# Holding 36 parts of the table in groups, storing 24 KB rows, and splitting the last step by blocks of the batch

## The chip, the cores and the metric

The kernel runs on one core of a Trainium2 chip. The metric is the device time of one execution in microseconds, the median of several runs. "Profile" means the record of one execution; its times count from the span's start. Engines: PE multiplies, ACT and DVE work on elements, POOL (GpSimd) issues the gathers, SP issues the stores; PSUM is the memory into which PE writes. A "packet" is one entry in the record of the 16 DMA engines; a store has one for each row of a partition, beside entries of 4 bytes that are left out here. The "seam" is the passage from the first stage to the second.

## The reference, cut to what matters

```python
emb = emb_table.at[0].set(0.0)              # 100001 x 128
e = emb[seq]                                # seq: 1024 x 50
prefix = jnp.cumsum(e, axis=1)
uF = prefix / denom[:, :, None]             # min(t, length)
mean, var = uF.mean(axis=0), uF.var(axis=0) # over the batch, for each step
y = (uF - mean) * lax.rsqrt(var + 1e-5) * gamma + beta
def step(v, x):
    v = v + (x - v) / 2.0
    spike = atan_spike(v - 1.0)             # 1 where v >= 1
    return v - spike, spike
_, spikes = lax.scan(step, v0, x_seq)       # 50 steps, in order
scores = spikes.mean(axis=0) @ emb.T        # 1024 x 100001, 410 MB
```

The first stage is the 50 steps: each gathers 1024 rows and ends in a count of spikes. The second multiplies the counts (1024 x 128) by the whole table and writes 410 MB. Almost nothing of it can start before the last step is done.

## The kernel before: the parts that the change touches

The table is cut into 98 "parts" of 1024 rows. A part is loaded (512 KB, 4 KB a partition), transposed by PE, split into a high and a low half (`hi`, `lo`; the result is the sum of two products), multiplied with eight blocks of 128 users, scaled out of PSUM by DVE and ACT in turn, and stored.

```python
CH = 4096            # a chunk: four parts, so a 16 KB row in each store
AHEAD = 8            # chunks loaded during the first stage: 32 parts
...
for c, (c0, w) in enumerate(chunks):
    ...
    for n in range(NB):                        # 8 blocks of 128 users
        o = op.tile([P, CH], F32, tag="o")     # three of these
        for q in range(parts[c]):
            ...product..., scale by 1/T into o[:, h0:h0+hw]
            if n == NB - 1: free.append(split.pop((c, q))[2]); ready()
        store(n, c0, o[:, :w])                 # on SP's queue
        if n in (2, 5): ready()                # transpose and split a part of the next chunk
    ...
    fetch(ahead.pop(0), rowp)                  # a later chunk, on ACT's queue
```

The last step works in two halves of 512 users, and block A (users 0 to 127) is multiplied first:

```python
x(halves[0]); x(halves[1])          # ACT: scale and shift
upper(0, 3, pt)                     # ACT: high half of part 3
step(halves[0])                     # DVE: 512 columns
spiked(countA, slice(0, P), vt)     # DVE: the counts of block A
for h, po in enumerate(pre):
    product(po, 0, 0, 0, h * BANK, BANK)
step(halves[1]) ...
```

## Time and profile before

| | before |
|---|---|
| time, median of 3 | 1660.91 us |
| span of the profile | 1587.5 us |
| second stage, first store to end | 513.5 to 1587.5 us |
| stored / fetched in the second stage | 409.6 / 34.4 MB |
| stores | 16 KB rows, 2 MB each, 12.8 us from issue to landing |

These are the queues of the page of the kernel before (packets, MB, share of the time of 16 DMA engines); q1 carries the stores and the first loads, q0 the gathers, q10 the fetches of the second stage:

```profile
q1 hardware_dynamic: 36256, 426.67, 63.9%
q0 software_dynamic: 12800, 26.24, 6.1%
q10 hardware_dynamic: 9292, 34.42, 6.1%
```

The prediction shows the rest: POOL paces the first stage, the bytes on the DMA engines the second. PE, at 78 to 85% in the second stage, is not far behind.

The profiled run was 71 us shorter than the timed ones.

### The profile page before, as it was taken

The page shows a single profiled execution, that of the slowest core. Times are in us where ns is not written, and L with a number is a line of the kernel's source. Part 1 is how long each engine was busy: PE and PEld are TensorE (multiplying, and loading weights), DVE is VectorE, ACT ScalarE, POOL GpSimd, SP SyncE. Part 2 cuts the span into 40 slices and gives each one's busy share as a digit, 9 for nine tenths or more (in the row PEclk, how much of TensorE's full clock was granted, in tenths as well). Part 3 has the DMA queues.
Part 4 walks back from the last instruction along what each step waited for, and adds up shares of the span by engine and source line. Part 5 has one row for each costly group of instructions (what it writes and reads, how often), then busy time and mean ns, then how long its engine had stood idle before and what let it go on. Part 6 is the DMA issues. An engine that isn't in the chain of part 4 may idle for free.

```text
span 1587.5 us, 12689 instructions
## 1 busy us (share of the span) xinstructions
PE 1137.8 (72%) x4532; PEld 804.7 (51%) x4532; DVE 939.4 (59%) x1162; ACT 631.6 (40%) x699; POOL 378.4 (24%) x406
## 2 busy tenths in 40 slices
PE   4555555555555977788888878788888788888884
PEld 2222222222233765566666666666666666666663
DVE  4777777777778654555555554555555545555553
ACT  2322222222233544444444444444444444444442
POOL 6777777777775000000000000000000000000000
PEclk9999999999965999999999999999999999999998
DMA  9522122221221999999999999999999999999998
GB/s 341 187 53 53 52 53 53 53 53 52 53 53 51 380 429 426 424 422 415 418 426 407 418 426 422 417 414 415 416 416 419 422 420 411 427 411 412 416 417 345
DMA packets 58410, 488.13 MB, mean 307 GB/s; under 512 B 12491, under 2 KB 13292, under 8 KB 33772
## 3 DMA queue, kind: packets, MB, share of 16 engines
q1 hardware_dynamic: 36256, 426.67, 63.9%
q0 software_dynamic: 12800, 26.24, 6.1%
q10 hardware_dynamic: 9292, 34.42, 6.1%
q8 instruction: 35, 0.57, 0.1%
q14 instruction: 27, 0.22, 0.0%
HBM read 77.69 MB, written 409.60 MB: 307 GB/s over the span
## 4 chain that ended last, share of the span: by engine, by line
DMA 52%; POOL 18%; issue 10%; PE 9%; DVE 7%; ACT 3%; DVEq 0%; SPq 0%; ACTq 0%; POOLq 0%
DMA scores<-o 48%; POOL e L191 18%; PE po L152 8%; DVE o L434 5%; DMA e<-in_L_rec_emb_table,idx 3%; ACT o L436 3%; PE pt L104 1%; PE pre L300 0%; ACT hi L136 0%; DVE s L330 0%; DVE bs L310 0%; DVE uF L309 0%; DMA idx<-in_r_seq 0%; ACT v L345 0%; DVE negv L353 0%
## 5 line engine op out<-in xcount | busy, mean ns | idle before, releaser
L434 DVE TENSOR_SCALAR o<-po 128x1024 f32<-128x1024 f32 x390 | 462.6, 1220 | 442.0 <-DMA scores<-o 338.5
L436 ACT ACTIVATE o<-po 128x1024 f32<-128x1024 f32 (+1 forms) x390 | 385.4, 1018 | 528.2 <-DMA scores<-o 347.4
L191 POOL DMA_INDIRECT e<-in_L_rec_emb_table,idx x400 | 377.7, 944 | 124.6 <-issue 116.4
L152 PE MATMUL po<-hi,countC 128*128 128x512 f32 x624 | 261.0, 418 | 81.7 <-ACT o L436 81.5
L300 PE MATMUL pre<-ident,e 128*128 128x128 f32 x400 | 155.9, 451 | 146.9 <-DMA e<-in_L_rec_emb_table,idx 145.0
L152 PE MATMUL po<-lo,countC 128*128 128x512 f32 x624 | 248.9, 399 | 0.0
L152 PE MATMUL po<-hi,countB 128*128 128x512 f32 x468 | 192.2, 411 | 14.4 <-ACT o L436 13.9
L300 PEld LDWEIGHTS pre<-ident,e 128*128 128x128 f32 x400 | 79.2, 200 | 241.7 <-DMA e<-in_L_rec_emb_table,idx 219.9
L152 PEld LDWEIGHTS po<-hi,countC 128*128 128x128 f32 x624 | 120.2, 193 | 133.5 <-ACT o L436 110.7
L152 PE MATMUL po<-lo,countB 128*128 128x512 f32 x468 | 186.9, 399 | 0.0
L104 PE MATMUL pt<-ident,rows 128*128 128x128 f32 x782 | 113.2, 292 | 70.5 <-ACT o L436 65.4
L104 PEld LDWEIGHTS pt<-ident,rows 128*128 128x128 f32 x782 | 96.4, 150 | 96.3 <-ACT o L436 79.8
L324 ACT ACTIVATE r<-mv,eps 128x1 f32<-128x1 f32 x50 | 14.8, 295 | 302.8 <-DVE mv L320 302.8
L152 PEld LDWEIGHTS po<-lo,countC 128*128 128x128 f32 x624 | 120.5, 193 | 22.1
L309 DVE SCALAR_TENSOR_TENSOR uF<-rlen,pre 128x512 f32<-128x512 f32 x100 | 68.3, 683 | 105.5 <-PE pre L300 105.5
L140 DVE TENSOR_TENSOR lo<-pt,hi 128x1024 fp32r<-128x1024 f32 x78 | 93.7, 1218 | 40.9 <-ACT hi L136 40.9
L152 PEld LDWEIGHTS po<-hi,countB 128*128 128x128 f32 x468 | 91.6, 196 | 41.7 <-ACT o L436 19.8
L152 PEld LDWEIGHTS po<-lo,countB 128*128 128x128 f32 x468 | 91.1, 195 | 18.2
L152 PE MATMUL po<-more,countC 128*128 128x512 f32 (+1 forms) x320 | 87.7, 413 | 16.1 <-ACT o L436 16.1
L136 ACT CAST hi<-pt 128x1024 fp32r<-128x1024 f32 x78 | 79.0, 1013 | 48.7 <-PE pt L104 48.7
L268 PE MATMUL sums<-s,ident_h 128*128 128x512 bf16 x98 | 49.6, 608 | 61.1 <-DVE s L330 61.1
L257 PE MATMUL pre<-zT,l 128*128 128x512 f32 x100 | 76.9, 771 | 19.7 <-DVE uF L309 19.5
(77 smaller groups left out, 942.7 us busy)
## 6 DMA issues: line engine op xcount, KB each, us to landing
scores<-o SPq DMA_DIRECT2D x190, 2048.0 KB, 12.8
rows<-in_L_rec_emb_table ACTq DMA_DIRECT2D x16, 2048.0 KB, 27.0
rows<-in_L_rec_emb_table SPq DMA_DIRECT2D x8, 2048.0 KB, 26.0
scores<-o SPq DMA_DIRECT2D x8, 848.5 KB, 14.6
e<-in_L_rec_emb_table,idx POOLq DMA_INDIRECT x400, 2.5
scores<-o SPq DMA_DIRECT2D x2, 1024.0 KB, 3.9
scores<-o SPq DMA_DIRECT2D x3, 512.0 KB, 2.7
scores<-o SPq DMA_DIRECT2D x2, 256.0 KB, 2.1
```

The source lines that it names most:

```text
L104: nc.tensor.transpose(pt[:, k0 : k0 + kw], rows[c][:kw, q * KQ + k0 // P, :], ident[:kw, :kw])
L136: nc.scalar.copy(vh, vp)
L140: nc.vector.tensor_tensor(vl, vp, vh.bitcast(F32), ALU.subtract)
L152: nc.tensor.matmul(po[:, :kw], lhsT=counts[n], rhs=part[:, k0 : k0 + kw], start=j == 0, stop=j == 1,)
L191: nc.gpsimd.indirect_dma_start(out=es[t][:, n * P : (n + 1) * P], out_offset=None, in_=table, in_offset=bass.IndirectOffsetOnAxis(ap=idx[: ...
L257: nc.tensor.matmul(pre[h], lhsT=l, rhs=zT[:, h * BANK : (h + 1) * BANK], start=t == 0, stop=False, skip_group_check=True,)
L268: nc.tensor.matmul(sums[h], lhsT=ident_h, rhs=s[:, h * BANK : (h + 1) * BANK], start=t == 0, stop=t == T - 2, skip_group_check=True,)
L300: nc.tensor.matmul(pre[h][:, k : k + P], lhsT=e[:, h * BANK + k : h * BANK + k + P], rhs=ident, start=False, stop=last, is_transpose=True, ...
L309: nc.vector.scalar_tensor_tensor(uF[:, cs], rlen[:, cs], 1.0 / (t + 1), pre[h], ALU.max, ALU.mult)
L324: nc.scalar.activation(r, mv[:, 1:2], AF.Sqrt, bias=eps)
L434: nc.vector.tensor_scalar_mul(o[:, h0 : h0 + hw], po[:, :hw], 1.0 / T)
L436: nc.scalar.mul(o[:, h0 : h0 + hw], po[:, :hw], 1.0 / T)
```

## The change

Its intent is to move fewer bytes in the second stage (36 parts held in place of 32), to move them in longer rows (24 KB), and to get the first store out sooner. To make room, the buffers are laid out as six groups of six parts, which are reused one by one: as pairs for the split halves, as output buffers, as places for later fetches. Chunks start narrow, since at first little room is free.

```diff
-CH = 4096
-AHEAD = 8
+GROUP = 6
+AHEAD = 6
+WIDTHS = [2, 2, 2, 3, 3, 3, 3] + 12 * [6] + [4, 4]
 ...
-                if T - 8 <= t < T - 2 and t % 2 == 0:
+                if t in (T - 8, T - 6):           # two parts prepared early, not three
 ...
-        pt = vp.tile([P, HALF], F32, tag="v0", name="pt_3")
-        turned(0, 3, pt)
-        x(halves[0])
-        x(halves[1])
-        upper(0, 3, pt)
-        step(halves[0])
-        spiked(countA, slice(0, P), vt)
+        warm = vp.tile([P, HALF], F32, tag="v0", name="warm")
+        for k in range(2 * KQ):
+            nc.tensor.transpose(warm[...], ident, ident)
+        vC = vp.tile([P, B - BANK - P], F32, tag="v1", name="vC")
+        groups = [
+            (slice(0, P), pre[0][:, :P], countA),
+            (slice(P, P + BANK), pre[1], countB),
+            (slice(P + BANK, B), vC, countC),
+        ]
+        for cs, vt, _ in groups: x(vt, cs)
+        cs, vt, first = groups[0]
+        step(vt, cs); spiked(first, cs, vt)
+        for cs, vt, _ in groups[1:]: step(vt, cs)
+        for cs, vt, c in groups[1:]: spiked(c, cs, vt)
 ...
-            if n in (2, 5):
+            if 2 <= n < NB - 1:
                 ready()
+            if n in (1, 4) and c >= MIDDLE and to_fetch < parts:
+                ...fetch(r, to_fetch, GROUP // 2)     # 1.5 MB, twice a wide chunk
```

## The prediction

> **What bounds the kernel now.** I read the page first: the 40 slices, the chain that ended last, and the DMA issues.
>
> ```profile
> DMA  9522122221221999999999999999999999999998
> GB/s 341 187 53 53 52 53 53 53 53 52 53 53 51 380 429 426 424 422 415 418 426 407 418 426 422 417 414 415 416 416 419 422 420 411 427 411 412 416 417 345
> ...
> DMA 52%; POOL 18%; issue 10%; PE 9%; DVE 7%; ACT 3%; DVEq 0%; SPq 0%; ACTq 0%; POOLq 0%
> ...
> scores<-o SPq DMA_DIRECT2D x190, 2048.0 KB, 12.8
> rows<-in_L_rec_emb_table ACTq DMA_DIRECT2D x16, 2048.0 KB, 27.0
> rows<-in_L_rec_emb_table SPq DMA_DIRECT2D x8, 2048.0 KB, 26.0
> ```
>
> There are two stages. For the first 13 slices (to about 510 us) the DMA engines are nearly idle after the first 55 us, in which eight chunks of the table are loaded. From slice 14 on they are full, at 407 to 429 GB/s, until the end. A 2 MB store lands 12.8 us after its issue although 2 MB at 420 GB/s take 5 us, so a backlog stands before the DMA engines.
>
> The first stage is paced by GpSimd's gathers. The timeline of that engine is the same at the beginning, under the load, as at its end:
>
> ```profile
> 30.73 0.94 POOL L191 DMA_INDIRECT e<-in_L_rec_emb_table,idx  x1 [0.30 <-issue]
> 31.97 0.94 POOL L191 DMA_INDIRECT e<-in_L_rec_emb_table,idx  x1 [0.30 <-issue]
> ...
> 502.63 0.94 POOL L191 DMA_INDIRECT e<-in_L_rec_emb_table,idx  x1 [0.30 <-issue]
> ```
>
> One gather every 1.25 us, 400 of them, 500 us; "issue" means that it waits for nothing shown. The loaded DMA engines at 30 us don't slow it.
>
> The busy time by stretches of the second stage shows the seam and the rest:
>
> ```profile
> 510.00:520.00 10.00, 7.26 (x24) 5.31 (x25) 7.45 (x11) 3.81 (x6) 0.00 (x0) 0.78 0.38 147
> 520.00:530.00 10.00, 10.00 (x50) 8.32 (x49) 6.09 (x6) 6.04 (x6) 0.00 (x0) 1.00 0.92 376
> ...
> 560.00:800.00 240.00, 187.96 (x841) 146.36 (x840) 123.45 (x106) 103.97 (x106) 0.00 (x0) 0.96 1.01 422
> 800.00:1300.00 500.00, 407.35 (x1776) 316.61 (x1777) 262.50 (x224) 220.84 (x223) 0.00 (x0) 0.95 1.01 418
> 1350.00:1560.00 210.00, 178.75 (x822) 138.94 (x821) 122.34 (x107) 101.13 (x104) 0.00 (x0) 1.00 0.99 417
> ```
>
> The columns are PE, its weight loads, DVE, ACT and POOL busy, then the granted clock, the DMA share and GB/s. DMA is at 0.99 to 1.01 throughout, PE at 78 to 85%, DVE at 51 to 58%. So the second stage lasts as long as its bytes take, and what can shorten it is fewer bytes, cheaper packets, or an earlier start.
>
> The seam itself, in the timeline, where "a" (the scale of the last step) is done at 508.79:
>
> ```profile
> 508.88 1.59 ACT L345 ACTIVATE v<-uF,hgb,a 128x512 f32<-128x512 f32 x2
> 510.42 1.00 ACT L136 CAST hi<-pt 128x1024 fp32r<-128x1024 f32 x1
> 510.51 0.70 DVE L348 SCALAR_TENSOR_TENSOR v<-negv,v 128x512 f32<-128x512 f32 x1 [1.72 <-ACT v L345]
> 511.24 0.29 DVE L279 SCALAR_TENSOR_TENSOR countA<-v,count 128x128 fp32r<-128x128 f32 x1
> ...
> 511.59 0.79 PE L152 MATMUL pre<-hi,countA 128*128 128x512 f32 x1 [3.40 <-DVE countA L279]
> ...
> 513.47 44.45 SPq L161 DMA_DIRECT2D scores<-o  x15
> ```
>
> The first product waits for countA, countA for a step over 512 columns, and that for both activations, although countA needs only 128 columns. The first store is issued at 513.47.
>
> One thing I can't explain: the timed runs take 1660.91 us, the profiled one 1589.44. I take the 71 us as the same for both kernels, so a saving in the profile is a saving in the time.
>
> **What the Trainium skill says.** "DMA: Bandwidth & Descriptors", section "Where 436 GB/s comes from", puts the ceiling of the 16 engines at 435 GB/s; the trace's 417 to 422 are 96% of it. Its section "Why small descriptors are slow (HBM only)" names a fixed cost for each packet. The packet records of this trace agree: medians of 159 ns for 4096 bytes, 311 for 8192 and 611 for 16384, a line of about 9 ns plus 0.0367 ns a byte. "HBM Reference", section "Specifications (TRN2)", gives about 358 GB/s for a core of a busy pair and says that a core alone exceeds it; 420 here is the core alone. "TensorE: Matmul & The Clock Gate", Part 1, says that the clock is halved after an idle window of about 3.4 us and full after a busy one. The clock records agree: half from 487 until 514.5 us, with PE continuously busy only from 511.59, and the products of 128x512 take 0.63 us before and 0.39 after.
>
> **The change, part by part.**
>
> 1. Fewer bytes in the second stage. Before, 8 chunks of 4 parts are loaded in stage one, 66 of 98 parts later. After, 36 parts are held and 62 come later. Four parts of 512 KB are 2.1 MB, at 420 GB/s 5.0 us. The extra bytes move to stage one, where DMA is idle and POOL wasn't delayed by the load: no cost. Gain 5.0 us.
>
> 2. Packets. In the stretch without fetches, 1350 to 1560, 5334 packets of 16384 bytes took 210 us on 16 engines: 630 ns each with the gap, against 602 for the bytes alone at 27.2 GB/s an engine (435/16), so 28 ns fixed. Beside fetches the gaps are filled by the other queue and only some 10 ns of it remain. The widths of the chunks are now 3x2, 4x3, 12x6 and 2x4 parts, with 8, 12, 24 and 16 KB packets. For 24 KB, 12288 packets save half a fixed cost each: 5 ns x 12288 / 16 = 3.8 us beside fetches, 14 ns and 10.8 us without. Eleven of the twelve wide chunks have fetches beside them, so I take 4.5 us. Against it the first seven chunks, none with fetches: 3072 packets of 8 KB cost half a fixed cost more than half a 16 KB packet does, 14 x 3072 / 16 = 2.7 us; 4096 packets of 12 KB a quarter, 7 x 4096 / 16 = 1.8 us. The sum is about nothing: between 3 us gained and 2 us lost. I enter 0.5 us gained.
>
> 3. The last step in three pieces. The activation for A covers 128 columns, about 0.39 us (the 128x128 activation of "l" took that) in place of 1.59 for two halves; the step over 128 columns about 0.29 in place of 0.70. So countA is ready at about 508.88 + 0.39 + 0.2 + 0.3 + 0.1 + 0.29 = 510.1, against 511.53. The order of PE's instructions shows sixteen transposes without use behind the counting matmuls, which end at 506.5: 16 x 0.24 = 3.8 us (eight took 1.91), up to 510.3, just before the first product. The busy window begins earlier, and the full clock should come at 511.1, one 3.4 us window before 514.5. The first store should leave near 511.6 in place of 513.47. After it, n = 0 has two parts in place of four, and PE makes a part in 0.93 us at full clock, faster than the 1.25 us that the DMA engines take to store it. The two stretches 510 to 530 moved 147 x 10 + 376 x 10 = 5.2 MB where 420 GB/s would move 8.4: 7.6 us lost. After, I expect 2 us before the first store and some 1.5 us of ramp. Gain 4 us.
>
> 4. New waits. The first chunks have two parts, and with three pairs of split buffers the second part of the next chunk is only transposed behind the first product of the last block. It needs the transposes (1.9), the cast (1.0) and the subtraction (1.2); PE has two products of 0.93 to cover the last two. That is a stall of about 1 to 2 us at the first two boundaries, at a time when little backlog stands. PE needs 2 x (7.4 + 1.9) = 18.6 us for such a chunk plus the stall, DMA 20: nearly even. Cost 1.5 us. From the third chunk on, five and then ten pairs are free, and the order of instructions shows the splits spread over blocks 2 to 6.
>
> Sum: 5.0 + 0.5 + 4.0 - 1.5 = 8 us in the middle; if gaps between stores beside fetches shrink too, some 4 us more. I take 10, so 1651 us.
>
> **Rivals.** First, PE becomes the bound in chunks 0 to 7, which now have no fetches: 24 parts at 10 us each for DMA, against 9.3 for PE at full clock. The stretch 1350 to 1560 speaks against it: no fetches there, DMA still 0.99, PE 85% busy. If the clock fell to 0.9 as in some stretches of 560 to 1300, PE would need 10.3 and the loss would be 24 x 0.3 = 7 us, leaving the time near 1658. Second, the long packets bring the whole 14 ns (10.8 us), because the queue is deeper with 3 MB stores and never empties: then about 1643. Third, the gain from the fetches is hidden because the held rows take the room of the output buffers, and the early stores of 1 MB don't keep DMA busy: a DMA share of 0.95 over chunks 0 to 6 (180 us) would cost 9 us, and the time would be as before. Fourth, the extra load delays the gathers: against it stands the 1.25 us pace at 30 us.
>
> **Range and chances.** Every term is under 1% of the time and the terms of loss are as large as those of gain, so over 2% (33 us) either way needs something that I don't see, most likely in the unexplained 71 us. Predicted 1651 us, range 1638 to 1662; faster by over 2%: 0.03, within 2%: 0.95, slower by over 2%: 0.02.
>
> **What would show it.** The bytes of the second hardware queue should fall from 34.42 to about 32.3 MB. The first store should leave at 511 to 512, and the clock in 510 to 520 should be above 0.78, with the DMA share of that stretch near 0.7. The DMA share from 520 to 700 should stay at 0.98 or more; if it is 0.95, the third rival is right, and with PE over 92% busy there, the first. The median packet of 24 KB should take about 911 ns. POOL should end at 503.6 as before. I would be wrong altogether if the time moved by more than the profile's span did.

## The result

| | before | after | ratio |
|---|---|---|---|
| | 1660.81 (4 runs) | 1649.11 (4 runs) | 0.9930 (0.9912 to 0.9947) |
| chip 9, run again | 1588.53 (9) | 1576.12 (5) | 0.9919 |
| chip 12, run again | 1589.05 (9) | 1576.17 (5) | 0.9918 |

Ratios are the mean time of one kernel's fast runs over that of the other's of the same rounds, so not quite the ratio of the medians.

The change saves 12 us, under 1%, wherever it is run. The level differs by 72 us between runs on different chips, for both kernels alike: on chips 3, 9 and 12 before takes 1588.5 to 1589.3 us, on chip 8 it takes 1661.1. Each chip was used in one session only, so chip and session can't be told apart; "kind of chip" below means which level was seen. By level, the profile of before came from the first kind, its timed runs and the profile of after from the second. So **the two pages must not be subtracted**: they would say that after is 59 us slower. The waits of POOL show what differs. In the profile of after (waiter, what it waited for, total us, times, longest):

```profile
POOL e L187 <- issue: 109.8, 360, 0.3
POOL e L187 <- remote: 64.2, 16, 4.4
```

On chip 9 the same kernel has the first of these two lines only, 114.0 us in 374 waits. So the gathers stop 16 times for about 4 us, 64 us in all; "remote" means that the profile has no record of what ended the wait. With one more stop of 5.5 us this is nearly the whole 71 us by which the scale of the last step comes later (579.15 against 508.29). The gathers are not where it begins: beside the stop at 79.1 us DVE had waited from 70.4 to 79.72, also for "remote", while POOL went on issuing and PE's eight transposes of that step stand in the record as ended at 71.1. The gathered data was on time (packets from 1.7 to 2.1 us after the issue, beside a stop as elsewhere). What DVE waited for, the record doesn't show. The comparisons below that rest on traces use chip 9, 3 or 12.

The page of after on chip 9, the DMA engines in 40 slices, the queues, and the issues (KB each, us from issue to landing):

```profile
DMA  9612121222121999999999999999999999999998
GB/s 337 249 52 54 52 54 52 54 52 54 52 54 44 391 411 419 420 399 424 424 428 430 430 426 421 422 422 415 425 429 417 416 423 416 430 425 421 384 423 353
...
q1 hardware_dynamic: 31984, 428.77, 64.8%
...
q10 hardware_dynamic: 8844, 32.33, 5.2%
...
scores<-o SPq DMA_DIRECT2D x96, 3072.0 KB, 20.0
...
rows<-in_L_rec_emb_table ACTq DMA_DIRECT2D x20, 1536.0 KB, 29.7
```

The fetches of the second stage fell by 2.1 MB. The second stage is full as before, with two slices that sag: 399 (the 18th, around 690 us) and 384 (the 38th, around 1470). A store now lands 20 us after its issue; three of 3 MB can stand in line.

The stretches of the same profile (PE, weight loads, DVE, ACT, POOL busy, granted clock, DMA share, GB/s):

```profile
510.00:520.00 10.00, 9.51 (x45) 7.57 (x46) 6.64 (x9) 5.82 (x8) 0.00 (x0) 1.00 0.71 279
520.00:530.00 10.00, 9.46 (x45) 7.38 (x44) 7.36 (x7) 5.34 (x6) 0.00 (x0) 1.00 0.93 382
560.00:690.00 130.00, 115.83 (x536) 89.41 (x535) 78.23 (x67) 65.33 (x67) 0.00 (x0) 0.99 1.00 416
690.00:700.00 10.00, 9.35 (x41) 7.43 (x40) 7.98 (x7) 5.57 (x7) 0.00 (x0) 1.00 0.77 322
800.00:1300.00 500.00, 407.96 (x1773) 321.00 (x1772) 261.78 (x222) 218.94 (x222) 0.00 (x0) 0.94 1.00 423
1465.00:1480.00 15.00, 12.05 (x45) 9.15 (x44) 7.09 (x6) 5.93 (x6) 0.00 (x0) 0.89 0.71 304
```

From 510 to 520 the clock is full and the DMA share 0.71, where before had 0.38. In the long stretch of the middle the rate is 423 in place of 418 GB/s. The two dips are in the fourth and the last line.

The seam of after on chip 9, in the timeline:

```profile
508.29 0.27 DVE L335 TENSOR_SCALAR a<-q,r,hgb 128x1 f32<-128x1 f32 x1
508.66 1.17 ACT L339 ACTIVATE pre<-uF,hgb,a 128x128 f32<-128x128 f32 x2
509.15 0.30 DVE L342 SCALAR_TENSOR_TENSOR pre<-negv,pre 128x128 f32<-128x128 f32 x1 [0.59 <-ACT pre L339]
509.49 0.29 DVE L275 SCALAR_TENSOR_TENSOR countA<-pre,count 128x128 fp32r<-128x128 f32 x1
...
509.92 0.47 PE L149 MATMUL sums<-hi,countA 128*128 128x512 f32 x1 [0.44 <-ACT pre L339]
...
510.23 0.40 PE L149 MATMUL sums<-lo,countA 128*128 128x512 f32 x1
...
511.29 0.84 SPq L158 DMA_DIRECT2D scores<-o  x2
```

The same steps of before, on the same chip:

```profile
508.45 0.27 DVE L339 TENSOR_SCALAR a<-q,r,hgb 128x1 f32<-128x1 f32 x1
...
511.52 0.79 PE L152 MATMUL pre<-hi,countA 128*128 128x512 f32 x1 [3.43 <-DVE countA L279]
...
513.41 1.31 SPq L161 DMA_DIRECT2D scores<-o  x2
```

From the start of the scale "a" to the first store it is now 3.0 us; before took 5.0 (508.45 to 513.41). Three quarters of that lie ahead of the first product, which starts 1.6 us after "a" in place of 3.1.

**A balance of the second stage.** I summed the packet records of chip 9's traces from the first store packet to the last one, each divided by 16 engines. Idle is the time in which fewer than 16 packets were in flight, overlap that in which more were; busy plus idle less overlap is the length.

| us | before | after | difference |
|---|---|---|---|
| store packets | 965.5 | 967.1 | +1.6 |
| fetch packets | 95.0 | 80.9 | -14.1 |
| instructions' own loads | 2.2 | 2.2 | 0 |
| idle, first 20 us | 3.2 | 1.8 | -1.4 |
| idle, last 10 us | 4.8 | 4.5 | -0.3 |
| idle, between | 7.2 | 10.2 | +3.0 |
| overlap | -6.9 | -6.0 | +0.9 |
| length | 1071.0 | 1060.8 | -10.2 |

With the first packet 2.1 us earlier (512.14 against 514.27) this is the whole 12.4 us. A second trace of the changed kernel, a1, has 965.9 for the store packets and 10.9 for the idle between, so both of these lines are good to about 1.3 us only; its fetch packets agree to 0.1. The packet means (ns):

| packet | before | after |
|---|---|---|
| store, 8 KB | 318 | 317 |
| store, 12 KB | | 469 |
| store, 16 KB | 617 | 619 |
| store, 24 KB | | 924 |
| fetch, 4 KB | 180.5 | 163.4 |

The long stores are hardly cheaper a byte than those of 16 KB (924 against one and a half times 617, 926). It is the fetch packets beside them that got shorter: 3.1% of their packets took over 400 ns before, 0.6% after.

### The profile page after: what moved, and what is told of

Its sections match the earlier page's. It is cut to its first block, busy times and chain, and to the rows that moved or that the text cites. A ratio compares the mean times of both kernels' runs of the same rounds, so it can differ in the third digit from the quotient of the medians.

```text
span 1646.4 us, 12555 instructions
## 1 busy us (share of the span) xinstructions
PE 1115.2 (68%) x4538; PEld 829.4 (50%) x4548; DVE 940.4 (57%) x1161; ACT 630.6 (38%) x700; POOL 379.3 (23%) x406
## 4 chain that ended last, share of the span: by engine, by line
DMA 48%; DVE 22%; another core or an unknown queue 10%; PE 9%; ACT 5%; issue 4%; POOL 1%; DVEq 0%; ACTq 0%; SPq 0%
DMA scores<-o 48%; PE po L149 8%; ACT o L456 4%; DVE bs L306 4%; DVE uF L305 4%; DVE v L342 3%; DVE s L326 3%; DVE negv L348 3%; DVE o L454 2%; POOL e L187 1%; DVE a L335 1%; DVE mv L316 1%; DVE q L332 0%; PE pt L119 0%
## 5 line engine op out<-in xcount | busy, mean ns | idle before, releaser
L149 PE MATMUL po<-pairs,countB 128*128 128x512 f32 x1168 | 313.9, 415 | 66.8 <-ACT o L456 49.6
L149 PEld LDWEIGHTS po<-pairs,countB 128*128 128x128 f32 x1168 | 225.4, 198 | 131.3 <-ACT o L456 64.4
L149 PE MATMUL po<-pairs,countC 128*128 128x512 f32 x876 | 238.2, 417 | 43.2 <-ACT o L456 43.0
L149 PEld LDWEIGHTS po<-pairs,countC 128*128 128x128 f32 x876 | 168.8, 199 | 89.3 <-ACT o L456 54.8
L305 DVE SCALAR_TENSOR_TENSOR uF<-rlen,pre 128x512 f32<-128x512 f32 x100 | 68.0, 680 | 180.5 <-remote 145.0
L142 DVE TENSOR_TENSOR pairs<-pt,pairs 128x1024 fp32r<-128x1024 f32 (+1 forms) x73 | 88.4, 1217 | 94.7 <-ACT pairs L141 94.7
L149 PE MATMUL po<-hi,countB 128*128 128x512 f32 x200 | 82.9, 414 | 19.2 <-ACT o L456 14.9
L149 PE MATMUL po<-lo,countB 128*128 128x512 f32 x200 | 80.4, 402 | 0.0
L149 PE MATMUL po<-pairs,countA 128*128 128x512 f32 (+1 forms) x292 | 73.5, 393 | 9.1 <-ACT o L456 9.1
L141 ACT CAST pairs<-pt 128x1024 fp32r<-128x1024 f32 (+1 forms) x73 | 73.6, 1008 | 15.0 <-PE pt L119 14.9
L149 PE MATMUL po<-hi,countC 128*128 128x512 f32 x150 | 63.2, 421 | 17.7 <-ACT o L456 17.7
```

Of the source, the lines that this page charges most:

```text
L141: nc.scalar.copy(vh, vp)
L142: nc.vector.tensor_tensor(vl, vp, vh.bitcast(F32), ALU.subtract)
L149: nc.tensor.matmul(po[:, :kw], lhsT=counts[n], rhs=part[:, k0 : k0 + kw], start=j == 0, stop=j == 1,)
L305: nc.vector.scalar_tensor_tensor(uF[:, cs], rlen[:, cs], 1.0 / (t + 1), pre[h], ALU.max, ALU.mult)
```

## The experiments

Each is a run of 5 rounds (before run again: 3) beside the kernel before on the same chip. The changed kernel took 1576.12 us on chip 9 and 1576.17 on chip 12; the differences below are to the first of these, for seam0 to the second. Nowarm, hold30, w4 and tailsp ran on chip 3, where the changed kernel was not run and before took 1589.25, 0.7 us more than on chip 9. Reckoned from before on their own chip, their differences would be 0.7 us smaller: 1.5, 6.0, 4.4 and -0.4 us. So these four are good to about 0.7 us.

### The kernel before, again (b0)

No edit.

> The kernel before, unchanged, to see its trace in the state of the timed runs. The changed kernel's profile has its first store at 582.1 us, with sixteen holes of 2 to 5 us in the gathers of GpSimd; the profile of before (1587.5 us) has no such hole and its first store at 513.5. Theory: in the timed runs (1660.8) the kernel before has the same holes, so a new profile spans about 1659 with the first store near 585 and the stage after it at 1074 us as before. Rival: its first stage is as in the old profile (513 us) and the stores take 1145 us instead, in which case the change would have traded one for the other. Ratio to before 1.000.

Measured: 1588.58 us, ratio 0.9999; its first store at 513.41 us, no hole. Here the state that the question was about was absent, so neither theory was tested. Only chip 8, in use later, brought 1661 us and the holes back; before was not profiled there.

### The changed kernel, again (a0, a1)

No edit; a0 on chip 9, a1 on chip 12.

> The changed kernel, unchanged, as the base for the edits in this call. Theory and rival alike: 1649 us within 2, ratio to before 0.993; first store near 582, 1064 us from there to the end.

> The changed kernel, unchanged, beside the next run, as its base and to see its ratio to before once more: 0.992 to 0.993 in either kind of session (1576 of 1588.5, or 1649 of 1660.8).

Measured: 1576.12 and 1576.17 us, ratios 0.9919 and 0.9918. The level of 1649 and the first store near 582 that were expected of a0 belong to the other kind of chip; the ratio holds on both.

### The last step in halves again (halves)

```diff
-        for cs, vt, _ in groups: x(vt, cs)
-        ...
+        vl = vp.tile([P, B], F32, tag="v1", name="vl")
+        for cs in halves: x(vl[:, cs], cs)
+        step(vl[:, halves[0]], halves[0])
+        spiked(countA, slice(0, P), vl[:, :P])
+        step(vl[:, halves[1]], halves[1])
+        for cs, c in ((slice(P, P + BANK), countB), (slice(P + BANK, B), countC)):
+            spiked(c, cs, vl[:, cs])
```

> The changed kernel with the last step again in two halves of 512 columns and v in one tile (the sixteen transposes and the rest of the change stay). Theory: from the scale of the last step to the first store 4.7 us as before in place of 2.7, so about 2 us longer, 1651. Rival: the first store comes earlier without use because the DMA engines catch up from the backlog; then 1649.

Measured: 1578.14 us, 2.0 longer; the first store at 512.97 in place of 511.29. Theory right: the delay at the seam was not made up later. By the packet records the second stage is as long as in a0, 1060.8 us both times.

### Without the sixteen transposes (nowarm)

```diff
-        warm = vp.tile([P, HALF], F32, tag="v0", name="warm")
-        for k in range(2 * KQ):
-            nc.tensor.transpose(warm[:, ...], ident, ident)
```

> The changed kernel without the sixteen transposes of the last step. Theory: the clock then is at half for the first products, which take 0.63 in place of 0.40 us until about 514.5; the first store leaves 0.5 us later and the ramp loses another 0.5 to 1 us: 1577 to 1577.5. Rival: the transposes do nothing for the time, since the vector engine's chain sets the first products; 1576.

Measured: 1578.37 us, 2.3 longer than on chip 9, 1.5 by the own chip's before; by the spans of the timed runs (median 1576.0 against 1574.3) it is 1.7. So the theory (1 to 1.5) is right or a little low. The products in its timeline:

```profile
510.04 0.77 PE L149 MATMUL sums<-hi,countA 128*128 128x512 f32 x1 [3.68 <-ACT pre L339]
510.60 0.63 PE L149 MATMUL sums<-lo,countA 128*128 128x512 f32 x1
511.03 0.63 PE L149 MATMUL sums<-hi,countA 128*128 128x512 f32 x1
```

They take 0.63 us until 514.4; in the changed kernel they take 0.40 from the second on. The first store leaves 0.6 us later (511.89) and the first 20 us hold 3.0 us of idle in place of 1.8: 1.8 us together. So sixteen transposes whose result nobody reads are worth 1.5 to 2.3 us on this kind of chip.

### Both undone (seam0)

Both edits together, on chip 12 beside a1.

> The changed kernel with both parts of the last step undone: two halves in place of three pieces, and no sixteen transposes. Alone they cost 2.0 and 2.3 us. Theory: they act on one chain one after the other (the counts come later, and then the first products run at half the clock), so they add up: 4.3 us longer than the run beside it. Rival: with the counts late the products wait for the vector engine, and the clock matters less: 3 us or under.

Measured: 1579.54 us, 3.4 longer than a1, on the same chip. So the last step's part of the change is worth 3.4 us (the narrow first chunk stays). Whether the two overlap stays open: 4.3 rests on nowarm, which is good to 0.7; the balance above has the same 3.5 us (2.1 for the first packet, 1.4 of idle).

### Holding 30 parts (hold30)

```diff
-AHEAD = 6
+AHEAD = 5
-        at = g if g < AHEAD else AHEAD - 2 + g % 2
+        at = g if g < AHEAD else AHEAD - 2 + (g - AHEAD) % 2
-                turns = [(rowp, "rows2", 6), (rowp, "rows3", 6), (op, "o", 6)]
+                turns = [(rowp, "rows2", 6), (rowp, "rows5", 6), (op, "o", 6)]
```

> The changed kernel holding 30 parts in place of 36 (five groups; 68 parts fetched later). Theory of bytes: six parts are 768 packets of 163 ns more, / 16 = 7.8 us longer, 1584. Rival: fetch bytes fill gaps of the stores and cost nothing; 1576 to 1578.

Measured: 1582.82 us, 6.7 longer. Fetch packets rose by 8.8 us; store packets fell by 1.6, no more than between a0 and a1. Bytes count nearly in full, 1.1 us a part, so the four parts of the change are worth about 4.5 us (an estimate: 6.7 x 4 / 6; with the own chip's before, 6.0, it is 4.0).

### Sixteen-kilobyte stores (w4)

```diff
-WIDTHS = [2, 2, 2, 3, 3, 3, 3] + 12 * [6] + [4, 4]
+WIDTHS = [2, 2, 2, 3, 3, 3, 3] + 2 * [6] + 17 * [4]
```

> The changed kernel with 17 chunks of four parts (16 KB rows) in place of ten of the twelve of six (and the two at the end): 60 parts and the end go back from 24 to 16 KB stores; held parts, fetches of 1.5 MB and last step stay. In the traces the 24 KB store packet takes 924 ns, one and a half of 16 KB 1.5 x 617 = 926: nothing. But a 4 KB fetch packet took 163 ns beside 24 KB stores and 181 beside 16 KB ones. Theory: the long stores pay through the fetches alone: fetch packets return to 180 ns, 7808 x 17 / 16 = 8 us longer, about 1584. Rival: the fetch packets got cheaper because the fetches are now 1.5 MB or spread over two points of a chunk; then they stay at 163 and the time at 1576.

Measured: 1581.20 us, 5.1 longer. A fetch packet took 175.6 ns, most of the way back to before's 180.5, and the fetches 6.0 us more; store packets took 2.0 us more, idle fell by 1.9. So the gain from the wide chunks is real, 5.1 us (4.4 by the own chip's before), and most of it stands in the fetches' packets, as the theory said, though its 8 us were too many. The same trace shows it beside itself: while the 24 KB stores of the two wide chunks that are left were under way, a fetch packet took 160.0 ns (2 of 768 over 400), afterwards 177.3 (212 of 7040); in a0 the figures for the same stretches are 159.9 and 163.8.

### Twelve-kilobyte stores from the same buffers (cut12)

```diff
+                if W == GROUP:
+                    store(n, q0 * HALF, o[:, : 3 * HALF])
+                    store(n, (q0 + 3) * HALF, o[:, 3 * HALF :])
```

> The changed kernel with each 24 KB row of the wide chunks stored in two DMAs of 12 KB rows, issued together, same buffers. Theory of the packets' fixed cost: two packets of 12 KB take 2 x 469 = 937 ns against 924 for one of 24 KB, 12288 x 13 / 16 = 10 us longer, 1659. Rival: what is paid is bytes, and gaps are filled by the fetches' queue; then 1649 to 1651. Third: the short packets let the fetches' small packets through faster, the stall of the stores at the last fetch (4 us of DMA idle in the changed kernel) goes, and the time falls to 1646.

Measured: 1588.43 us, 12.3 longer: all that the change had gained. Store packets cost 11.4 us more (two of 469.5 ns against one of 924.4), as the fixed cost said, and idle 4.5 more; the fetch packets took 1.9 less and 2.2 more were overlapped. The third theory is refuted: the stall at the last fetch grew. SP's longest wait for that fetch was 16.3 us in place of 13.9, and the DMA engines stood nearly still from 1460 to 1467 us. But the fetch packets here took only 159.6 ns, less than beside 24 KB. So "the longer the stores, the shorter the fetches" is not the rule; 16 KB stores are the worst of the three beside fetches, and why that is so stays open. A rival is untested: w4 changed the packets' length and the bytes that can stand in line together. Before and w4 have three stores of 2 MB in line; the changed kernel and cut12 have 9 MB, with packets of 24 and of 12 KB, and short fetch packets both times.

### The last fetch on the stores' queue (tailsp)

In the changed kernel SP waits once for a fetch to land, as its waits show from 1440 to 1500 us:

```profile
SPq L158 <- DVE o L454: 43.3, 8, 7.8
SPq L158 <- DMA rows<-in_L_rec_emb_table: 13.9, 1, 13.9
```

It is the last, partial part: 673 packets of 512 bytes on ACT's queue. In that wait the DMA engines idle about 4 us (the dip near 1475). Before had the same wait with 7.5 us.

```diff
             if full:
-                engine.dma_start(
+                nc.sync.dma_start(
 ...
             if rest:
-                engine.dma_start(out=r[:rest, full, :], ...)
+                nc.sync.dma_start(out=r[:rest, full, :], ...)
```

> The changed kernel with the last partial part of the table (673 packets of 512 bytes) fetched on the stores' queue in place of ACT's. Theory: on ACT's queue these packets take turns with 24 KB store packets of 0.92 us, some 40 turns an engine, so the fetch lands 40 us late, the stores' sequencer waits 13.9 us for its semaphore and the DMA engines idle about 4 us near 1475 us. In line with the stores there are no turns: that dip goes, 3 to 4 us shorter, about 1572.5. Rival: the dip is made up from the backlog or moves elsewhere; 1576.

Measured: 1576.47 us, no gain. Its SP waits from 1400 us on:

```profile
SPq L158 <- DVE o L454: 139.9, 25, 8.4
SPq L158 <- ACT o L456: 8.0, 11, 1.5
```

The wait for the fetch is gone and so is its dip, but there are new ones at 1497 to 1504 (DMA share 0.74 to 0.79) and, weaker, 1534 to 1539 (0.92), and the idle of the whole stage is 16.8 us as against 16.5. From 1490 to 1545 DVE and ACT wait up to 5.5 us at a time for a store to free an output buffer; that the next store is then late because six parts have to be computed first is my reading, not shown. The rival was right.

### The last part held from the start (tailheld), and rows stored in two halves (best1)

```diff
+    def fetch_tail():                       # called in the first stage
+        r = const.tile([P, full + 1, D], F32, tag="tail", name="tail")
+        nc.sync.dma_start(...)
```

and for best1, on top of it:

```diff
+            early = (c == MIDDLE and n < 2) or n == NB - 1 or c + 2 == len(WIDTHS)
+            cut = W // 2 if early and W > 3 else 0
 ...
+                elif cut and q + 1 == q0 + cut:
+                    store(n, q0 * HALF, o[:, : cut * HALF])
 ...
-                store(n, q0 * HALF, o[:, : ...])
+                store(n, (q0 + cut) * HALF, o[:, cut * HALF : ...])
```

> The changed kernel with the last partial part of the table (345 KB, 3 KB a partition) loaded in the first stage and held, so that no transfer of 512-byte packets runs beside the stores. With that transfer on the stores' queue the wait of 13.9 us went and the time did not change (1576.47 against 1576.12): new idle of about 4 us stood at 1495 to 1540 us, where computing waits for output buffers. Theory A: the idle of the DMA engines near the end is set by the three output buffers and the block of six parts, whatever the last fetch does; only the bytes are saved, 673 x 27 / 16 = 1 us: 1575. Theory B: the transfer cost its stall of 4 us, and putting it on the stores' queue cost the same in another way (small packets in line): 1572.

> The same as the last, with some rows of the wide chunks stored in two halves, the first as soon as its parts are there: the first two blocks of the first wide chunk, the last block of every chunk, and all of the last chunk but one. Theory A (the DMA engines run dry while six parts are computed): the dips of 2.5 us near 692 and of some 4 us between 1495 and 1540 and the small ones at the chunks' ends shrink, about 5 us less than the run before it: 1570. Rival: twelve-kilobyte packets cost 15 ns a pair more in 19 blocks x 128 / 16 = 2 us, and the dips are set by the buffers' release: 1575 or more.

Both ran on chip 8, the slower kind, where before took 1661.08 us: 1651.88 (ratio 0.9941, 0.9929 to 0.9953) and 1655.01 (0.9959, 0.9945 to 0.9972). The changed kernel's own ratio is 0.993 on such a chip, so neither total is better. Their second stages lasted 1060.1 and 1064.5 us by the packet records, against 1060.8 in a0 and 1061.9 in the profile of after, which is of their kind. In tailheld's profile the stage began 4.7 us later than in that one, and the difference arose before the last step's scale (583.79 against 579.15), among the holes: its total can't show whether the 1 us of theory A was saved. The 4 us of theory B were not. The idle of the DMA engines was 17.1 and 17.6 us: in best1 the dip at the first wide chunk shrank (1.6 us in place of 2.1) and others appeared, and the fetch packets rose to 172 ns, which cost more than the dips gave. I found no version that beats the changed kernel.

## Why the prediction was right or wrong

**The total and the range were right**: 1651 was said and 1649.11 measured, in a range of 1638 to 1662, within 2% at 0.95. That the 71 us would be the same for both kernels held: 11.7 us were saved where they are present, 12.4 where they are not. The worked sum was 8 us, though; the step from 8 to 10 leaned on "gaps" that were not worked out, and the right total owes something to errors that cancel: step 2 was too low and step 4 too cheap.

**Step 1, fewer bytes: right.** 5.0 us were said, 4.0 to 4.5 follow from hold30.

**Step 2, packets: wrong.** "The sum is about nothing", 0.5 us, was entered; w4 shows 5.1. The step failed in its model: it gave store packets a fixed cost, expected the gain there, and gave the fetch packets none. The fixed cost it used, 28 ns with the gap, is not the 9 ns of its own line through the medians; cut12 measures 14.6 ns for a 24 KB packet cut in two. Between 16 and 24 KB the store packets save little (2.0 us of w4's 5.1), and the gain stands mostly with the fetches, whose packets went from 180.5 to 163.4 ns. The narrow chunks cost less than said: by the packet means against 617 ns for 16 KB, 1.4 us for the 8 KB packets and 1.5 for those of 12 KB (an estimate), where 2.7 and 1.8 were said. The median of 24 KB, said as 911, was 912 ns; the prediction looked at medians, while the effect was in the few long packets of another queue. What it called "gaps between stores beside fetches", with "some 4 us more", has the right size and not the right place.

**Step 3, the last step: right in mechanism, slightly too large.** 4 us were said, seam0 gives 3.4. The first store was said for near 511.6 and left at 511.29; the clock in 510 to 520 was 1.00 and the DMA share 0.71, as asked for. The transposes took 3.4 us in place of 3.8 and the clock was full from 509.12 in place of 511.1. On the slower kind of chip they did not hold it:

```profile
575.18 3.56 PE L363 MATMUL warm<-ident 128*128 128x128 f32 x16 [0.24 <-DVE negv L291]
...
580.77 0.47 PE L149 MATMUL sums<-hi,countA 128*128 128x512 f32 x1 [2.04 <-ACT pre L339]
...
582.07 0.63 PE L149 MATMUL po<-lo,countA 128*128 128x512 f32 x1
```

The pause behind them was 2.0 us here and 0.44 in a0. The clock records of this profile have full clock for 3.41 us from 578.48, half from 581.90 and full again from 585.31, and the products took 0.63 us until 585. Those of tailheld and best1 have the same fall, from 580.17 and 580.95. So what the transposes are worth there was not measured.

**Step 4, new waits: right in size at best, wrong in place.** Stalls of 1.5 us at the first two boundaries were said; no dip of the DMA engines stands there. Idle between the ends grew by 3.0 us (3.7 in a1), at the first wide chunk (about 2.3 us near 692, where, as I read it, six parts must be computed before the first 3 MB store leaves) and at the last fetch (about 4 us; before has a smaller stall of this kind).

The three gains that were measured by undoing them, 4.5 + 5.1 + 3.4, come to 13.0 us, or 11.8 by the own chips' before (4.0, 4.4 and 3.4), beside 12.4 for the whole. That this fits is no proof: w4 leaves the two first wide chunks, the narrow chunks (a loss of 2.9 us by the estimate above) and some 2.4 us of shorter fetch packets (180.5 to 175.6 ns) as they are, and nothing undoes the new idle alone; tailsp took away its largest piece and gained nothing.

**The rivals.** PE as the bound: PE was busy 115.83 of 130 us from 560 to 690 (89%), with DMA at 1.00, so no. The long packets' full 10.8 us: no, 5.1. Early stores that don't fill the engines: no, 1.00 there, and 0.98 over the whole stretch that the prediction named, 520 to 700. Delayed gathers: no, the last one was issued at 502.48 us, on the same chip before at 502.55.

## What to carry to other kernels

Here the DMA engines were the bound, and what removed their work or started it sooner showed in the time: bytes moved into the idle first stage counted nearly in full. A removed stall did not count at all; the idle came back at other places. Look at the packets of every queue when a store's size changes, and at their tail rather than at the median. And before subtracting two profiles, run the old kernel again on the same chip in the same session: here the two pages differ by 59 us in the wrong direction.

## What the Trainium skill lacked or had wrong

- "DMA: Bandwidth & Descriptors", section "Where 436 GB/s comes from", says that for HBM to SBUF transfers the HBM side, about 358 GB/s, binds. The sentence does not name the condition that both cores of a pair are busy. The one core in use here moves 416 to 423 GB/s over its long stretches, with stores to HBM for the most part; "HBM Reference", section "Specifications (TRN2)", which says that a core alone is well above that share, agrees.
- The same page, section "Why small descriptors are slow (HBM only)", has a fixed cost for each packet and says nothing of what two queues do to each other; the page's section on queues says that an engine takes turns between them packet by packet, but not what a packet then costs. Measured: 24 KB store packets 924 ns, 16 KB 617, 12 KB 469, 8 KB 317; a 4 KB fetch packet 163 ns in the kernel with 24 KB stores, 176 to 181 with 16 KB ones, 160 with 12 KB ones. I found no page that has this.
- The same page, section "SWDGE vs HWDGE vs iDMA", has packets of at most 4096 bytes preferably, for what GpSimd builds; the gathers' packets here have 4096, which agrees. For the queues of SP and ACT I found no figure; their packets recorded here have up to 24576. A fetch of 673 packets of 512 bytes beside such stores kept the stores' sequencer waiting 13.9 us.
- "TensorE: Matmul & The Clock Gate", Part 1, has the clock halved after an idle window of about 3.4 us. In the profile on record a pause of 2.0 us (578.74 to 580.77) was enough: the 3.41 us of its clock records that hold this pause beside 1.4 us of work were followed by half the clock, and the products ran at 0.63 us again from 582. That sixteen transposes without use in front of the seam, 3.4 us long, gain 1.5 to 2.3 us (nowarm) agrees with the page.
- I found no page that tells of such a difference between chips (or sessions): the kernel before takes 1588.5 to 1589.3 us on three chips and 1661.1 on a fourth; the changed kernel's trace at the slower level has 16 stops of about 4 us in the gathers of GpSimd, whose cause it doesn't show.
